# Graph convolution and sparse attention on one core: exponentials at the end of their slots, first-block scores and residual additions one slot later, more values on ScalarE in the last pair

## The chip, the core and the metric

The kernel runs on one core of a Trainium2 chip. A core has TensorE (PE) for matrix products and transposes, VectorE (DVE), ScalarE (ACT), GpSimd (POOL) and SyncE (SP), each with its own queue of instructions, and DMA engines that all queues share. The metric is the device time of one launch in microseconds (us), the median of several runs.

## The reference

`x` has 8 batches of 2048 nodes with 256 features; `adj` is a 2048 by 2048 adjacency matrix, sparse, with its densest rows and columns at the front. Layer 0 is a graph convolution with two linear layers and batch norms, layer 1 an attention with 4 heads that looks only at neighbours. Each is added to its input and layer-normalised. The change touches layer 1 and the end of layer 0 (the second batch norm, the addition and the layer norm), all of which the attention part of the kernel does.

```python
def _L1_gnn_ref(h, W, adj):
    qkv = h @ W
    qkv = qkv.reshape(Bn, Nn, 3, H, HEAD_DIM).transpose(2, 0, 3, 1, 4)
    q, k, v = (qkv[0], qkv[1], qkv[2])
    mask = jnp.where(adj == 0, -jnp.inf, 0.0)
    scores = jnp.einsum('bhid,bhjd->bhij', q, k) / np.sqrt(HEAD_DIM) + mask
    attn = jax.nn.softmax(scores, axis=-1)
    out = jnp.einsum('bhij,bhjd->bhid', attn, v)
    return out.transpose(0, 2, 1, 3).reshape(Bn, Nn, OUT_DIM)
# --- layer 0 ---
x = _layernorm(x + _L0_gnn_ref(x, adj, ...), axis=-1)
# --- layer 1 ---
x = _layernorm(x + _L1_gnn_ref(x, L1_gnn_W, adj), axis=-1)
```

## The kernel before

Everything is in 32-bit floats. The first part of the program builds lists of neighbours and computes layer 0 up to its second batch norm; its result lies in DRAM as `y_d`. The rest is the function `attention`, which this document is about.

**Two kinds of work.** The batches are taken in four pairs. For each pair a *projection* makes queries, keys and values; and a *gather loop* over 132 tiles does the sparse attention of the blocks of 128 query rows 1 to 15. Block 0, whose rows have the most neighbours, is done densely inside the projection. The projection of pair 0 runs alone first. Then the gather loop of pair p runs together with the projection of pair p+1, and the last pair's gather loop runs alone. That makes 528 tiles in all.

**The gather loop.** One turn of the loop is called a slot; slot n issues, in this order: `score(n+4)`, `weigh_values(n+3)`, `add_up(n)`, `gather(n+10)`, then what the projection has for this slot, then what is due later (`finish_block`, `out_stats`, `out_root`, `out_shift`, `emit`).
- `gather` has POOL start an indirect DMA that brings 128 rows of keys and values of both batches into `kg` (10 buffers), and for a tile of left-over edges a second one that brings queries (`qg`). The first tile of a block also loads its queries on SP (`qb`).
- `score` has DVE multiply queries and keys (L1100) and sum per head (L1102), and ACT take the exponential (L1107) into `pw`; for tiles of left-over edges DVE makes a one-hot matrix `oh` (L1110).
- `weigh_values` multiplies the values by the exponentials: on DVE as one instruction (L1126), or, where n % 5 is in `ON_ACT`, that is 1 or 3, on ACT as eight (L1121).
- `add_up` has PE add the weighted values to the block's sums in PSUM (L1140).
- `finish` has DVE divide by the sums (L992 to L996) and POOL add the input (L1002); the layer norm of the result follows.

**The projection.** It works by units of 512 rows of one batch, eight to a pair. Unit k starts at slot s = 14 k (9 k for pair 0, which runs alone), and `at` puts each of its functions into a slot. `bn` (ACT, L853) applies layer 0's batch norm at s. `norm` at s+1 and s+2 transposes half of y on PE into a PSUM tile `pm` (L863), and DVE adds x (L867) and takes statistics (L809, L811). `root`, `shift` and `apply` (POOL, DVE, ACT) do the layer norm, `turn` (PE L889, ACT L894) transposes the result. Then, for each of four tiles of 128 rows, starting at u = s+9 plus 0, 3, 7 or 10: `keys_values` at u (PE L911, ACT L925 and L926), `queries` at u+1 (PE L911, ACT L930), `turn_keys` at u+2 (PE L935, ACT L939), `scores0` of block 0 at u+3 (PE L948, two `pm` tiles), `mask0_scores` at u+4 (DVE L957, ACT L962) and `weigh` at u+6 (PE L970). `store` (SP L979, L983) writes keys, values and queries to DRAM at the last u+3; the next pair's first gather needs them.

**What sets the order.** The order of each queue is the order in which the program text issues its instructions: nothing is rearranged, and the projection's functions stand in their slot in the order in which `at` was called (an earlier unit's first). Each queue runs by itself and waits by semaphores for what an instruction reads, and for the buffer that it writes to be free. The buffers that matter here: `pm`, three PSUM tiles shared by all of the projection's PE work; `pw` and `wv`, five each; `s`, three; `kt` and `p0`, two.

Of the kernel before, what the change touches and what calls it, by code (L numbers as in the profile page):

```python
# [8 lines left out]
F32 = mybir.dt.float32  # L9
# [3 lines left out]
AF = mybir.ActivationFunctionType  # L13
# [4 lines left out]
NHEADS = 4  # L18
# [19 lines left out]
def tile_gcn_then_masked_attention(  # L38
# [15 lines left out]
    nc = tc.nc  # L54
    ENG = mybir.EngineType
    PSUM = bass.MemoryType.PSUM
    P = 128
    B, N, D = x.shape
# [9 lines left out]
    TPC = CH // P  # L68
# [372 lines left out]
    with tc.tile_pool(name="l0", bufs=1, side="right", reuse_waits="tile") as lp, tc.tile_pool(  # L441
# [126 lines left out]
        for n in range(len(tiles)):  # L568
            t, r, col, e = tiles[n]
# [262 lines left out]
    def attention():  # L832

        with ExitStack() as st:
# [4 lines left out]
            ps_m = enter(tc.tile_pool(name="ps_m", bufs=3, space=PSUM, reuse_waits="tile"))  # L839
            enter(tc.manual_schedule(engines=ALL4))  # L840

            x1, yt, x1t, ln, lo, kvr, qr, kt, q0, s0, p0, po0 = ({} for _ in range(12))

            def load(b, c):
                yt[b, c] = ip.tile([P, NO, CH], F32, name="yt")
# [9 lines left out]
                        bias=sh2[:, o : o + 1], scale=sc2[:, o : o + 1],  # L855
                    )

            def norm(b, c, half):
                pm = ps_m.tile([P, IT, D], F32, name="pm")
                for i in range(IT):  # L860
                    r0 = (IT * half + i) * P
                    for o in range(NO):
                        nc.tensor.transpose(  # L863
                            pm[:, i, o * P : (o + 1) * P], yt[b, c][:, o, r0 : r0 + P], ident
                        )
                t = x1[b, c][:, IT * half : IT * (half + 1)]
                nc.vector.tensor_add(t, pm, t)  # L867
                if not half:
                    ln[b, c] = LayerNorm(ip, x1[b, c])
                ln[b, c].stats(range(IT * half, IT * (half + 1)))  # L870
# [152 lines left out]
            def projection(p, step):  # L1023

                slots = {}

                def at(s, f, *args):
                    slots.setdefault(s, []).append((f, args))

                units = [(b, c) for b in range(p * G2, (p + 1) * G2) for c in range(NCH)]  # L1030
                for k, (b, c) in enumerate(units):
                    s = k * step
                    at(max(0, s - step), load, b, c)
                    at(s, bn, b, c)
                    at(s + 1, norm, b, c, 0)
                    at(s + 2, norm, b, c, 1)
                    at(s + 3, root, b, c)
                    at(s + 4, shift, b, c)
                    at(s + 5, apply, b, c, 0)
                    at(s + 6, apply, b, c, 1)  # L1040
                    at(s + 7, turn, b, c, 0)
                    at(s + 8, turn, b, c, 1)
                    if not c:
                        at(s + 9, first_queries, b)
                    for i in range(TPC):
                        u = s + 9 + (step * i) // TPC
                        at(u, keys_values, b, c, i)
                        at(u + 1, queries, b, c, i)
                        at(u + 2, turn_keys, b, c, i)
                        at(u + 3, scores0, b, c, i)  # L1050
                        at(u + 4, mask0_scores, b, c, i)
                        at(u + 6, weigh, b, c, i)
                    at(u + 3, store, b, c)
                    if c == NCH - 1:
                        at(u + 7, lambda b=b: finish(b, 1, 0, po0.pop(b)[:, None]))
                        at(u + 9, out_stats, b, 1, 0)
                return slots

            slots = projection(0, 9)
# [6 lines left out]
            NG = len(tiles)  # L1066
            LEAD = 10
            AHEAD = 4
            ON_ACT = (1, 3)
            kg, qg, qb, oh, pw, wv, po = ({} for _ in range(7))  # L1070

            def load_q(p, t):
                qb[p, t] = ep.tile([P, G2, D], F32, name="qb", bufs=3)
# [21 lines left out]
            def score(n):  # L1095
                p, g = divmod(n, NG)
                t, r, col, e = tiles[g]
                q = qb[p, t] if e < 0 else qg.pop(n)
                pr = ep.tile([P, G2, D], F32, name="pr")
                nc.vector.tensor_mul(pr, q, kg[n][:, :, :D])  # L1100
                s = ep.tile([P, G2, NHEADS], F32, name="s", bufs=3)
                nc.vector.tensor_reduce(  # L1102
                    s.rearrange("p b h -> p (b h)"),
                    pr.rearrange("p b (h e) -> p (b h) e", e=HD), AX.X, ALU.add,
                )
                pw[n] = ep.tile([P, G2, NHEADS], F32, name="pw", bufs=5)
                nc.scalar.activation(pw[n], s, AF.Exp, bias=padb[:, col : col + 1])  # L1107
                if e >= 0:
                    oh[n] = ep.tile([P, P], F32, name="oh", bufs=4)
                    nc.vector.tensor_scalar(  # L1110
                        oh[n], iota_q1, qi1[:, e : e + 1], None, op0=ALU.is_equal
                    )

            def weigh_values(n):
                wv[n] = ep.tile([P, G2, NHEADS * VW], F32, name="wv", bufs=5)
                k, w = kg.pop(n), pw.pop(n)
                if n % 5 in ON_ACT:
                    for b in range(G2):
                        for h in range(NHEADS):
                            hs = slice(h * VW, (h + 1) * VW)  # L1120
                            nc.scalar.activation(  # L1121
                                wv[n][:, b, hs], k[:, b, D:][:, hs], AF.Copy,
                                scale=w[:, b, h : h + 1],
                            )
                    return
                nc.vector.tensor_mul(  # L1126
                    wv[n].rearrange("p b (h e) -> p b h e", e=VW),
                    k[:, :, D:].rearrange("p b (h e) -> p b h e", e=VW),
                    w[:, :, :, None].to_broadcast([P, G2, NHEADS, VW]),
                )  # L1130
# [22 lines left out]
            def at(n, f, *args):  # L1153
                later.setdefault(n, []).append((f, args))
# [3 lines left out]
                gather(n)  # L1158
            for n in range(AHEAD):
                score(n)  # L1160
                if n:
                    weigh_values(n - 1)
            for n in range(NALL_G):
# [12 lines left out]
                    f(*args)  # L1176
                for f, args in later.pop(n, ()):
                    f(*args)
                if r == ELL[t] + CAP[t] - 1:
                    at(n + 1, finish_block, p, t)  # L1180
                    at(n + 3, out_stats, p * G2, G2, t)
                    if t % TPC == TPC - 1:
                        for b in range(p * G2, (p + 1) * G2):
                            u = n + 4 + 2 * (b % G2)
                            at(u, out_root, b, t // TPC)
                            at(u + 1, out_shift, b, t // TPC)
                            for half in range(2):
                                at(u + 2 + half, emit, b, t // TPC, half)
# [19 lines left out]
    class Layer1Input:  # L1208
# [37 lines left out]
        def turn_y(self, b, c, half, pm):  # L1246
            y = self.yt[b, c]
            for i in range(IT):
                r0 = (IT * half + i) * P
                for o in range(NO):  # L1250
                    nc.tensor.transpose(
                        pm[:, i, o * P : (o + 1) * P], y[:, o, r0 : r0 + P], ident
                    )
# [310 lines left out]
```

## Time and profile before

| what | value |
|---|---|
| median of 3 runs (lowest to highest) | 2800.45 us (2800.2 to 2802.91) |
| the profiled execution's own time | 2723.71 us |
| its span | 2721.9 us |
| busy PE, DVE, ACT, POOL over the span | 84%, 70%, 45%, 52% |
| granted TensorE clock, mean | 0.921 |
| L1100 and L1102, DVE, a tile | 0.70 and 0.69 us |
| L1126, weighting on DVE, a tile | 0.73 us |
| L1121, weighting on ACT, one of eight | 0.34 us |
| L1107, exponential on ACT | 0.30 us |
| first gather, last gather | 1303.0 us, 2689.9 us |

The page and the views of one trace are read so: busy times are sums over an engine's instructions, and instructions of one engine may overlap slightly at their ends, so that eight L1121 take about 2.0 us from the first start to the last end. A wait is the idle time just before an instruction, with the instruction that ended it. All times count from the start of the span of this one execution, which was shorter than the runs without a profile.

### The profile page before, as it was taken

The page shows a single profiled execution, that of the slowest core. Times are in us where ns is not written, and L with a number is a line of the kernel's source. Part 1 is how long each engine was busy: PE and PEld are TensorE (multiplying, and loading weights), DVE is VectorE, ACT ScalarE, POOL GpSimd, SP SyncE. Part 2 cuts the span into 40 slices and gives each one's busy share as a digit, 9 for nine tenths or more (in the row PEclk, how much of TensorE's full clock was granted, in tenths as well). Part 3 has the DMA queues.
Part 4 walks back from the last instruction along what each step waited for, and adds up shares of the span by engine and source line. Part 5 has one row for each costly group of instructions (what it writes and reads, how often), then busy time and mean ns, then how long its engine had stood idle before and what let it go on. Part 6 is the DMA issues. An engine that isn't in the chain of part 4 may idle for free.

```text
span 2721.9 us, 29515 instructions
## 1 busy us (share of the span) xinstructions
PE 2295.2 (84%) x8636; PEld 1364.2 (50%) x8636; DVE 1914.8 (70%) x3801; ACT 1227.6 (45%) x3664; POOL 1418.5 (52%) x1481
## 2 busy tenths in 40 slices
PE   6998989889998999799688887888887988966675
PEld 2444444344443444466466665656665666644443
DVE  7966343345439666432688889788798888889997
ACT  6210111011101555355466755766765666755554
POOL 3225435344312577200656657656567566677775
PEclk7999989899989999899798998999998999988777
DMA  9867556467633673332977879878888878889985
GB/s 363 289 253 296 214 199 243 163 223 250 224 110 131 263 263 138 135 117 86 334 267 276 308 269 336 315 252 301 310 304 294 315 261 305 289 281 335 320 310 181
DMA packets 235723, 689.02 MB, mean 253 GB/s; under 512 B 25632, under 2 KB 91680, under 8 KB 213024
## 3 DMA queue, kind: packets, MB, share of 16 engines
q0 software_dynamic: 109248, 442.68, 46.2%
q1 hardware_dynamic: 124000, 227.58, 23.0%
q10 hardware_dynamic: 2304, 16.78, 1.5%
q8 instruction: 71, 1.16, 0.2%
q14 instruction: 100, 0.82, 0.1%
HBM read 556.67 MB, written 130.29 MB: 252 GB/s over the span
## 4 chain that ended last, share of the span: by engine, by line
PE 49%; DVE 24%; ACT 12%; issue 7%; DMA 4%; POOL 3%; SPq 1%; ACTq 0%; POOLq 0%; DVEq 0%
PE pa L588 15%; PE pm L911 7%; PE pa L679 7%; DVE pr L1100 6%; PE ph L469 5%; ACT wv L1121 5%; PE pa L426 4%; DVE s L1102 4%; DVE wv L1126 4%; PE po L1140 3%; ACT x L825 2%; PE pm L948 2%; DVE ln_st L809 1%; PE pm L863 1%; DVE x L867 1%
## 5 line engine op out<-in xcount | busy, mean ns | idle before, releaser
L1084 POOL DMA_INDIRECT kg<-kv_d,idx x528 | 566.9, 1074 | 172.1 <-issue 91.1
L1140 PE MATMUL po<-wv,ident 128*128 128x260 f32 x1472 | 449.2, 433 | 100.6 <-ACT wv L1121 66.1
L588 PE MATMUL pa<-e,wt 128*128 128x512 f32 x928 | 437.6, 620 | 11.3 <-DVE e L327 10.7
L1121 ACT ACTIVATE wv<-kg,pw 128x65 f32<-128x65 f32 x1688 | 425.1, 337 | 0.1
L911 PE MATMUL pm<-wq,x1t 128*128 128x512 f32 (+1 forms) x1024 | 406.2, 521 | 10.4 <-DVE p L957 8.5
L1140 PEld LDWEIGHTS po<-wv,ident 128*128 128x128 f32 x1472 | 291.8, 213 | 209.7 <-ACT wv L1121 106.8
L1102 DVE TENSOR_REDUCE s<-pr 128x8 f32<-128x512 f32 x528 | 362.1, 686 | 18.3
L1107 ACT ACTIVATE pw<-s,padb 128x8 f32<-128x8 f32 x528 | 157.7, 299 | 392.3 <-DVE s L1102 391.6
L588 PEld LDWEIGHTS pa<-e,wt 128*128 128x128 f32 x928 | 180.9, 200 | 225.6 <-issue 206.6
L1126 DVE TENSOR_TENSOR wv<-kg,pw 128x520 f32<-128x520 f32 x317 | 229.9, 725 | 53.8 <-ACT pw L1107 53.0
L1100 DVE TENSOR_TENSOR pr<-qb,kg 128x512 f32<-128x512 f32 x368 | 257.8, 701 | 7.0 <-DMA kg<-kv_d,idx 6.8
L911 PEld LDWEIGHTS pm<-wq,x1t 128*128 128x128 f32 x1024 | 190.5, 198 | 117.4 <-issue 68.3
L1002 POOL TENSOR_TENSOR x<-z,x 128x256 f32<-128x256 f32 x128 | 111.6, 890 | 241.6 <-DVE z L996 241.3
L1140 PE MATMUL po<-wv,oh 128*128 128x260 f32 x640 | 200.6, 440 | 37.8 <-ACT wv L1121 24.5
L523 POOL DMA_INDIRECT e<-xs_d,idx x116 | 114.7, 989 | 161.1 <-PE pa L588 122.1
L1090 POOL DMA_INDIRECT qg<-q_d,idxq x160 | 164.3, 1027 | 48.8 <-issue 46.9
L1140 PEld LDWEIGHTS po<-wv,oh 128*128 128x128 f32 x640 | 129.4, 217 | 97.9 <-ACT wv L1121 43.6
L948 PE MATMUL pm<-q,kt 64*128 64x128 f32 x1024 | 95.0, 305 | 80.9 <-ACT kt L939 80.1
L304 POOL DMA_INDIRECT av<-in_adj_dram,fidx x116 | 113.3, 977 | 82.7 <-DVE wgt L298 32.6
L957 DVE SCALAR_TENSOR_TENSOR p<-mask,pm 128x256 f32<-128x256 uint8 x256 | 95.3, 413 | 82.4 <-PE pm L948 82.4
L970 PEld LDWEIGHTS po<-kvr,p 128*128 128x128 f32 x1024 | 131.6, 191 | 24.1 <-issue 15.8
L970 PE MATMUL po<-kvr,p 128*128 128x65 f32 x1024 | 129.4, 269 | 9.2 <-ACT p L962 9.2
(196 smaller groups left out, 3478.3 us busy)
## 6 DMA issues: line engine op xcount, KB each, us to landing
kv_d<-kvr SPq DMA_DIRECT2D x32, 1032.0 KB, 8.0
e<-h_d SPq DMA_DIRECT2D x28, 1024.0 KB, 8.1
e<-in_adj_dram SPq DMA_DIRECT2D x16, 1024.0 KB, 19.6
xt<-in_x_dram SPq DMA_DIRECT2D x16, 1024.0 KB, 7.6
xs_d<-xt ACTq DMA_DIRECT2D x16, 1024.0 KB, 7.7
y_d<-y SPq DMA_DIRECT2D x32, 512.0 KB, 2.7
yt<-y_d SPq DMA_DIRECT2D x32, 512.0 KB, 9.1
x<-in_x_dram SPq DMA_DIRECT2D x32, 512.0 KB, 12.9
```

Of the source, the lines that this page charges most:

```text
L588: nc.tensor.matmul(pa[:, c, :], w, xg[n].t[:, c * CH : (c + 1) * CH], start=(r == 0), stop=(r == ELL[t] + CAP[t] - 1),)
L679: nc.tensor.matmul(py, w[:, f, :], t[:, f, :], start=(f == 0), stop=(f == 1))
L911: nc.tensor.matmul(pm, x1t[b, c][:, d, i * P : (i + 1) * P], rhs(d), start=(d == 0), stop=(d == ND - 1),)
L970: nc.tensor.matmul(po0[b][:, h, :], p[:, h % 2, h // 2, :], heads(kvr[b, c][:, i, D:])[:, h, :], start=(j == 0 and h == 0), stop=(j == NT ...
L1084: nc.gpsimd.indirect_dma_start(out=kg[n].rearrange("p b e -> p (b e)"), out_offset=None, in_=kv_d[p][:], in_offset=bass.IndirectOffsetOnAx ...
L1090: nc.gpsimd.indirect_dma_start(out=qg[n].rearrange("p b e -> p (b e)"), out_offset=None, in_=q_d[p][:], in_offset=bass.IndirectOffsetOnAxi ...
L1100: nc.vector.tensor_mul(pr, q, kg[n][:, :, :D])
L1102: nc.vector.tensor_reduce(s.rearrange("p b h -> p (b h)"), pr.rearrange("p b (h e) -> p (b h) e", e=HD), AX.X, ALU.add,)
L1107: nc.scalar.activation(pw[n], s, AF.Exp, bias=padb[:, col : col + 1])
L1121: nc.scalar.activation(wv[n][:, b, hs], k[:, b, D:][:, hs], AF.Copy, scale=w[:, b, h : h + 1],)
L1126: nc.vector.tensor_mul(wv[n].rearrange("p b (h e) -> p b h e", e=VW), k[:, :, D:].rearrange("p b (h e) -> p b h e", e=VW), w[:, :, :, None ...
L1140: nc.tensor.matmul(po[p, t][:, b, : NHEADS * VW], lhs, w[:, b, :], start=(r == 0), stop=(r == ELL[t] + CAP[t] - 1),)
```

## The change

Four things are altered, all in `attention`.

1. `norm` is split. `turn_y` (the transposes) keeps its slots s+1 and s+2; the addition and its statistics come one slot after it, at s+2 and s+3, and everything of the unit that follows, from `root` to the stores and the end of block 0, one slot later than before. A transposed half is kept in `ys` until then.
2. `scores0`, `mask0_scores` and `weigh` come at u+4, u+5 and u+7, so the scores follow two slots after the keys are turned, not one.
3. The exponential is taken out of `score` into `exps`, which is issued at the end of the slot, after the weighting of the tile before, the gather and the projection's and later work.
4. For the last pair (n at least 396) `weigh_values` uses `LAST_ON_ACT`: ACT weighs where n % 5 is 0, 2 or 4, DVE where it is 1 or 3.

```diff
@@ -839,7 +839,7 @@
             ps_m = enter(tc.tile_pool(name="ps_m", bufs=3, space=PSUM, reuse_waits="tile"))
             enter(tc.manual_schedule(engines=ALL4))
 
-            x1, yt, x1t, ln, lo, kvr, qr, kt, q0, s0, p0, po0 = ({} for _ in range(12))
+            x1, yt, x1t, ln, lo, kvr, qr, kt, q0, s0, p0, po0, ys = ({} for _ in range(13))
 
             def load(b, c):
                 yt[b, c] = ip.tile([P, NO, CH], F32, name="yt")
@@ -855,16 +855,18 @@
                         bias=sh2[:, o : o + 1], scale=sc2[:, o : o + 1],
                     )
 
-            def norm(b, c, half):
-                pm = ps_m.tile([P, IT, D], F32, name="pm")
+            def turn_y(b, c, half):
+                pm = ys[b, c, half] = ps_m.tile([P, IT, D], F32, name="pm")
                 for i in range(IT):
                     r0 = (IT * half + i) * P
                     for o in range(NO):
                         nc.tensor.transpose(
                             pm[:, i, o * P : (o + 1) * P], yt[b, c][:, o, r0 : r0 + P], ident
                         )
+
+            def norm(b, c, half):
                 t = x1[b, c][:, IT * half : IT * (half + 1)]
-                nc.vector.tensor_add(t, pm, t)
+                nc.vector.tensor_add(t, ys.pop((b, c, half)), t)
                 if not half:
                     ln[b, c] = LayerNorm(ip, x1[b, c])
                 ln[b, c].stats(range(IT * half, IT * (half + 1)))
@@ -1032,28 +1034,29 @@
                     s = k * step
                     at(max(0, s - step), load, b, c)
                     at(s, bn, b, c)
-                    at(s + 1, norm, b, c, 0)
-                    at(s + 2, norm, b, c, 1)
-                    at(s + 3, root, b, c)
-                    at(s + 4, shift, b, c)
-                    at(s + 5, apply, b, c, 0)
-                    at(s + 6, apply, b, c, 1)
-                    at(s + 7, turn, b, c, 0)
-                    at(s + 8, turn, b, c, 1)
+                    for half in range(2):
+                        at(s + 1 + half, turn_y, b, c, half)
+                        at(s + 2 + half, norm, b, c, half)
+                    at(s + 4, root, b, c)
+                    at(s + 5, shift, b, c)
+                    at(s + 6, apply, b, c, 0)
+                    at(s + 7, apply, b, c, 1)
+                    at(s + 8, turn, b, c, 0)
+                    at(s + 9, turn, b, c, 1)
                     if not c:
-                        at(s + 9, first_queries, b)
+                        at(s + 10, first_queries, b)
                     for i in range(TPC):
-                        u = s + 9 + (step * i) // TPC
+                        u = s + 10 + (step * i) // TPC
                         at(u, keys_values, b, c, i)
                         at(u + 1, queries, b, c, i)
                         at(u + 2, turn_keys, b, c, i)
-                        at(u + 3, scores0, b, c, i)
-                        at(u + 4, mask0_scores, b, c, i)
-                        at(u + 6, weigh, b, c, i)
+                        at(u + 4, scores0, b, c, i)
+                        at(u + 5, mask0_scores, b, c, i)
+                        at(u + 7, weigh, b, c, i)
                     at(u + 3, store, b, c)
                     if c == NCH - 1:
-                        at(u + 7, lambda b=b: finish(b, 1, 0, po0.pop(b)[:, None]))
-                        at(u + 9, out_stats, b, 1, 0)
+                        at(u + 8, lambda b=b: finish(b, 1, 0, po0.pop(b)[:, None]))
+                        at(u + 10, out_stats, b, 1, 0)
                 return slots
 
             slots = projection(0, 9)
@@ -1066,8 +1069,8 @@
             NG = len(tiles)
             LEAD = 10
             AHEAD = 4
-            ON_ACT = (1, 3)
-            kg, qg, qb, oh, pw, wv, po = ({} for _ in range(7))
+            ON_ACT, LAST_ON_ACT = (1, 3), (0, 2, 4)
+            kg, qg, qb, oh, sc, pw, wv, po = ({} for _ in range(8))
 
             def load_q(p, t):
                 qb[p, t] = ep.tile([P, G2, D], F32, name="qb", bufs=3)
@@ -1103,18 +1106,22 @@
                     s.rearrange("p b h -> p (b h)"),
                     pr.rearrange("p b (h e) -> p (b h) e", e=HD), AX.X, ALU.add,
                 )
-                pw[n] = ep.tile([P, G2, NHEADS], F32, name="pw", bufs=5)
-                nc.scalar.activation(pw[n], s, AF.Exp, bias=padb[:, col : col + 1])
+                sc[n] = s
                 if e >= 0:
                     oh[n] = ep.tile([P, P], F32, name="oh", bufs=4)
                     nc.vector.tensor_scalar(
                         oh[n], iota_q1, qi1[:, e : e + 1], None, op0=ALU.is_equal
                     )
 
+            def exps(n):
+                col = tiles[n % NG][2]
+                pw[n] = ep.tile([P, G2, NHEADS], F32, name="pw", bufs=5)
+                nc.scalar.activation(pw[n], sc.pop(n), AF.Exp, bias=padb[:, col : col + 1])
+
             def weigh_values(n):
                 wv[n] = ep.tile([P, G2, NHEADS * VW], F32, name="wv", bufs=5)
                 k, w = kg.pop(n), pw.pop(n)
-                if n % 5 in ON_ACT:
+                if n % 5 in (LAST_ON_ACT if n >= (NP - 1) * NG else ON_ACT):
                     for b in range(G2):
                         for h in range(NHEADS):
                             hs = slice(h * VW, (h + 1) * VW)
@@ -1158,6 +1165,7 @@
                 gather(n)
             for n in range(AHEAD):
                 score(n)
+                exps(n)
                 if n:
                     weigh_values(n - 1)
             for n in range(NALL_G):
@@ -1176,6 +1184,8 @@
                     f(*args)
                 for f, args in later.pop(n, ()):
                     f(*args)
+                if n + AHEAD < NALL_G:
+                    exps(n + AHEAD)
                 if r == ELL[t] + CAP[t] - 1:
                     at(n + 1, finish_block, p, t)
                     at(n + 3, out_stats, p * G2, G2, t)
```

## The prediction

> **What bounds the kernel now.** I read the page first for shares and slices, then the busy times by stage (one row per stretch of the span), then the waits of each engine in the stages that the change touches, then single episodes in the timeline. Attention starts near 1110 us. By the first gather (1303.0 us) the projection of pair 0 is done; three pairs are then gathered while the next pair is projected (1303 to 2396), and the last pair is gathered alone (2396 to 2709).
>
> ```profile
> core 0: us, PE busy (x) PEld busy (x) DVE busy (x) ACT busy (x) POOL busy (x), PEclk, DMA share, GB/s
> 1110.00:1303.00 193.00, 171.19 (x981) 116.43 (x979) 59.96 (x175) 96.64 (x226) 14.43 (x54) 0.96 0.36 124
> ...
> 1303.00:2396.00 1093.00, 903.42 (x4456) 657.27 (x4458) 927.34 (x1931) 702.14 (x2394) 695.42 (x793) 0.93 0.84 296
> 2396.00:2709.00 313.00, 208.98 (x588) 127.87 (x586) 285.73 (x542) 160.97 (x620) 231.60 (x229) 0.79 0.84 294
> ```
>
> Columns: length, then busy us of PE, PE's weight loads, DVE, ACT, POOL, then TensorE's clock, DMA share, GB/s. In the first stretch PE is the bound (171 of 193 us). In the three shared pairs DVE (927 of 1093, 85%) and PE (903, 83%) are close to each other and neither is full: about 166 us of DVE time is waiting. In the last pair DVE is the bound (286 of 313, 91%). DVE's waits, in the shared pairs:
>
> ```profile
> engine line waited for: us in total, times, longest us
> DVE x L867 <- PE pm L863: 61.2, 42, 3.5
> DVE wv L1126 <- ACT pw L1107: 52.7, 45, 4.7
> DVE lo_nm L819 <- POOL lo_rs L140: 7.2, 7, 2.0
> DVE pr L1100 <- DMA kg<-kv_d,idx: 6.3, 1, 6.3
> ```
>
> Two waits hold 114 of those 166 us: the residual addition waiting for its transposes, and the weighting of values waiting for its exponentials. PE and ACT, in the same stretch:
>
> ```profile
> PE pm L948 <- ACT kt L939: 79.6, 52, 4.5
> PE pm L863 <- DVE p L957: 37.7, 21, 2.9
> ...
> ACT pw L1107 <- DVE s L1102: 246.0, 125, 11.3
> ACT kvr L925 <- PE pm L911: 95.9, 53, 4.8
> ```
>
> ACT stands 246 us at an exponential, first in its slot, while DVE still forms the sum; PE stands 80 us at first-block scores whose keys ACT copies one slot earlier. One episode shows how they lock:
>
> ```profile
> 1482.49 0.74 DVE L957 SCALAR_TENSOR_TENSOR p<-mask,pm 128x256 f32<-128x256 uint8 x2
> ...
> 1482.96 0.66 PE L863 MATMUL pm<-ident,yt 128*128 128x128 f32 x4 [0.85 <-DVE p L957]
> ...
> 1483.65 0.69 DVE L867 TENSOR_TENSOR x<-pm,x 128x512 f32<-128x512 f32 x1 [0.42 <-PE pm L863]
> ```
>
> PE can't transpose until DVE's masking frees a `pm` buffer, and DVE's next instruction waits for exactly that transpose.
>
> **What the Trainium skill says.** "PSUM — Partial Sum Buffer", section "Engine vs sequencer instructions": the queues of ScalarE, VectorE and GpSimd are strictly first in, first out. The episode agrees: behind L867 all of DVE stood still. So the place of an instruction in its queue is a cost by itself, and that is what most of this change alters. "Perfetto Trace Analysis", section "Optimizing Scalar/DVE Operations": with DVE saturated, moving work to ScalarE may make sense. The last pair's row (DVE 91%, ACT 51%) is that case. No other page is needed.
>
> **The change, part by part.** The profiled execution took 2723.71 us (span 2721.9); the runs' median is 2800.45, 77 us more, which the profile doesn't explain. I carry the change in us over to the median.
>
> (a) Residual addition a slot later (`turn_y` at s+1, `norm` at s+2, and all that follows a slot later). The transposes are now a whole slot ahead of their reader. A slot lasts 1093/396 = 2.76 us; transposes of a half took 0.66 us after at most one masking. So the 61.2 us wait should nearly go; I keep 5. But `pm` has three buffers, and one is now held across a slot boundary. Following the new order through a unit of 14 slots, a new same-slot wait appears: two score buffers and the second transposed half fill all three, so `keys_values` of the third tile can start only after DVE's second addition of that slot. Queued behind it on PE are the next slot's value sums, whose slack is three slots; on ACT the copies of keys and values. That leads to (c).
>
> (b) First-block scores two slots after their keys. PE's 79.6 us at L948 should almost vanish. PE isn't the fuller engine, and DVE loses only 4.2 us to PE at the masking now, so I book nothing. What replaces it late is the same-slot buffer wait (masking, then the next `pm`), which exists before too (37.7 and 8.5 us of PE).
>
> (c) Exponentials at the end of the slot. No instruction is added. ACT gets to the slot's values and copies without the 246 us stand; but each exponential now sits behind that slot's copies from PE. DVE's L1126 of the next slot needs it 1.37 us (product and sum, starts 0.7 apart) after that slot begins. Worst chain, from (a): addition ends, PE 1.98, ACT copies 0.72, exponential 0.30, hand-overs 0.1 = 3.1 us, against DVE's statistics, product and sum, 2.2 us: 0.9 us late. Behind a masking with a query product: 1.03 + 0.37 + 0.30 + 0.1 = 1.8 against 1.37: 0.4 late. Behind masking with keys turned and `turn`: 0.6 late. A key-value product whose slot is PE's fullest (sums, weighting, scores and product, 4.5 us at the page's durations) comes 1.3 late; two others 0.3. Sum per unit 0.9 + 2x0.4 + 0.6 + 1.3 + 2x0.3 = 4.2 us, and only the 60% of tiles that DVE weighs feel it: 2.5 us, x24 units = 60 us against 52.7 now: +7. Ends: 10 us (ACT's head start hides all: -43) and 120 us (+67, twice my lateness).
>
> (d) The stores of keys, values and queries, the block-0 finish and its statistics move a slot too. On SP the store goes from s+22 to s+23; loads of the next unit keep their slots and come first in the first stretch. At a pair's end the first gather needs the last store, and POOL already stands there: 5.9, 3.5 and 6.9 us before the three later pairs, followed before the last pair by DVE 5.06 us behind POOL's addition (L1002). A slot later costs POOL up to 2.8 us more; the gather is six slots ahead of its score, 16 us, less 6.3 landing, less the stand: little is left. I take +2 each, +6 (0 to +10).
>
> (e) Last pair: positions 0, 2, 4 of five instead of 1, 3. Of tiles 396 to 527, 79 go to ACT instead of 53: 26 fewer L1126 on DVE, which cost 0.61 us start to start (0.72 in the row): -16 to -19. ACT takes 26 x 1.92 to 2.02 = 50 to 53 more, from 161 to 213 of some 300: hidden, two neighbouring ones take 4.4 of two slots' 4.7. What is late next is POOL: 231.6 busy, plus 42 of pauses between gathers that nothing ends and 12 of 0.3 us ones, is 286 of 313; the rest, 23, is waiting for DVE's quotients. So POOL gives way by at most 27, and DMA is 84 to 91% busy there. I take -12 (-19 to -3). The final chain stays: the last tile moves to ACT (2.0 for 0.7) but no longer waits for its neighbour's.
>
> (f) First stretch: PE's work is unchanged and it is the bound; 0 (-4 to +5).
>
> (g) Pass-through. With 61 us of stalls gone DVE would be 88% busy, PE 86%, DMA 88%, so other waits will lengthen. I return 15 of (a)'s 56.
>
> Sum: (a) -56+15, (c) +7, (d) +6, (e) -12, (f) 0 = -40 us; I allow (b) and ACT's head start -6, so -46: 2678 for the profiled execution, 2754 for the median.
>
> **Rivals.** R1, the exponentials eat the gain: (c) reaches its bad end of 120 us and (a) is only balanced: -56+15+67+6-12 = +20 at worst, middle of the way about -9: 2791. For it: the new order puts 4 key-value and 4 query copies per unit ahead of an exponential; PE is 83% busy, so seldom early. Against: ACT now starts a slot's work about 1.4 us earlier.
>
> R2, slower: a closed loop DVE masking or addition, PE product, ACT copy, exponential, DVE weighting, one turn per slot. Place: the seven late slots per unit; with 60% on DVE that is 7 x 0.6 x 24 = 101 weightings. It decides once these wait (52.7 + 46 + 7)/101, about 1.0 us each, on average; my list gives 0.6. At 1.5 us: 152 - 60 = +92, so -46+92 = +46: 2846. For it: only three `pm` buffers, one now held longer. Against: the lateness isn't carried over, as PE has 9.6 us of work in the 11 us between two such locks.
>
> R3, only the last pair fails to gain, because POOL's gathers bind it: -34: 2766. It lies inside the forecast's range.
>
> That the change doesn't do what it says is excluded: the instruction order of the changed program shows each of the moves, and ScalarE loads one table in both.
>
> **How the numbers follow.** Forecast (with R3) 0.62; R1 0.16; R2 0.22. A measurement of this kernel tells about 0.2% from no change, 5.6 us. The forecast's cases all lie beyond that on the fast side; R1 splits 0.09 faster, 0.06 same, 0.01 slower. So faster 0.71, same 0.06, slower 0.23. The forecast's own range, from the ends of (a) to (f), is 2720 to 2785; with R1 and the near part of R2, leaving out about 0.15 above and 0.04 below, 2717 to 2816.
>
> **What would show it.** Right: L867 waiting for L863 under 10 us; PE at L948 waiting for keys under 20; ACT's wait for the sum well under 246; the stretch of shared pairs 1050 to 1065 us with DVE about 88% busy; the last pair about 300 with L1126 there at some 58 and POOL's waits for quotients under 23. Wrong: L1126 waiting for exponentials above 115 us (R1) or 155 (R2), PE waiting for the second addition at L911, or the last pair as long as before. A stand at the pairs' ends that grows by more than 10 us in all would break (d).

## The result, and the profile after

The changed kernel takes 2805.88 us (median of 20 runs, 2794.02 to 2814.62), the kernel before 2800.99 us in the same series (20 runs, 2795.55 to 2811.58): a ratio of 1.0014, 95% interval 1.0002 to 1.0026. Five microseconds were lost where 46 were forecast as a gain.

The kernel before takes about 2724 us in some series of runs and 2786 to 2802 us in others; its profile, on which the prediction rests, is of the first kind, the profile after (span 2802.3 us) of the second, and the 77 us that the prediction left unexplained are most likely this difference. So ratios below always stand between runs of one series, and times of the two profiles are not subtracted from each other.

The busy times by stage of the changed kernel, with the columns of the prediction's first fence:

```profile
0.00:1304.00 1304.00, 1184.11 (x3594) 578.81 (x3594) 699.68 (x1324) 359.96 (x642) 494.56 (x460) 0.95 0.57 209
1304.00:2480.00 1176.00, 944.37 (x4435) 682.92 (x4436) 922.38 (x1920) 715.17 (x2384) 690.57 (x791) 0.90 0.80 275
2480.00:2803.00 323.00, 205.29 (x608) 126.39 (x608) 275.73 (x533) 224.31 (x847) 233.82 (x232) 0.81 0.84 291
```

The first stretch is as long as before: the first gather starts at 1303.9 us, before at 1303.0. In the last pair 227 more instructions run on ACT than before (847 for 620, in a window 10 us longer); 208 of them are the new share of ACT, eight for each of 26 tiles. The shared pairs are the trouble: DVE does 922 us of work in 1176, 78%, where the prediction wanted 88% of 1050 to 1065. The waits of DVE in that stretch:

```profile
DVE wv L1133 <- ACT pw L1119: 180.1, 97, 10.3
DVE wv L1133 <- issue: 13.0, 8, 4.4
...
DVE lo_nm L819 <- POOL lo_rs L140: 5.2, 7, 1.4
```

The residual addition (now L869) no longer appears: that wait is gone, as meant. But the weighting (L1133, before L1126) waits 180 us for exponentials, 97 times and up to 10.3 us; in the profile before it was 52.7 us, at most 4.7. Ten of the 97, the eight longest among them, contain a stand of ACT whose releaser the trace doesn't know (last section). These ten hold 58 of the 180 us; the longest of the others is 4.2 us. ACT and PE in the same stretch:

```profile
ACT kvr L927 <- PE pm L913: 207.3, 71, 10.1
ACT p L964 <- DVE p L959: 82.5, 57, 2.6
ACT pw L1119 <- DVE s L1105: 56.5, 36, 10.8
```

```profile
PE pm L913 <- DVE x L869: 36.2, 16, 4.3
...
PE pm L891 <- DVE p L959: 34.0, 20, 2.8
```

ACT's 246 us at the exponential fell to 57. In exchange ACT now stands 207 us at the copies of keys and values, waiting for PE's products (before 96), and 82.5 us at the exponentials of block 0, waiting for DVE's masks (before 18); the moved exponential is queued behind both. One episode in the timeline of the changed kernel shows it (start, length, instruction; in brackets the idle time before it):

```profile
1503.58 1.98 PE L913 MATMUL pm<-wq,x1t 128*128 128x512 f32 x4
1504.06 0.69 DVE L1105 TENSOR_REDUCE s<-pr 128x8 f32<-128x512 f32 x1
...
1505.60 0.37 ACT L927 COPY kvr<-pm 128x256 f32<-128x256 f32 x1 [5.40 <-PE pm L913]
...
1506.13 0.31 ACT L1119 ACTIVATE pw<-s,padb 128x8 f32<-128x8 f32 x1
...
1506.48 2.03 ACT L1128 ACTIVATE wv<-kg,pw 128x65 f32<-128x65 f32 x8
...
1508.41 0.61 ACT L964 ACTIVATE p<-p 128x512 f32<-128x512 f32 x1
1508.93 0.36 ACT L932 ACTIVATE qr<-pm 128x256 f32<-128x256 f32 x1
...
1509.20 0.28 ACT L1119 ACTIVATE pw<-s,padb 128x8 f32<-128x8 f32 x1
...
1509.51 0.70 DVE L1133 TENSOR_TENSOR wv<-kg,pw 128x520 f32<-128x520 f32 x1 [1.75 <-ACT pw L1119]
```

The sum for the last exponential is ready at 1504.75. Its exponential starts at 1509.20, 4.45 us later: ACT first stands for PE's product, then does the copies, the exponential of the tile before, that tile's eight values (2.03 us), the block-0 exponentials (one instruction) and a copy of queries. DVE has meanwhile done the next product and sum, and stands for 1.75 us. In the old place the exponential would have been queued ahead of the eight values, the block-0 exponential and the copy of queries, which belong to its slot, but still behind the copies of keys and values of the slot before.

### The profile page after: what moved, and what is told of

It is laid out like the page before. It is cut to its first block, busy times and chain, and to the rows that moved or that the text cites. A ratio compares the mean times of both kernels' runs of the same rounds, so it can differ in the third digit from the quotient of the medians.

```text
span 2802.3 us, 29764 instructions
## 1 busy us (share of the span) xinstructions
PE 2333.8 (83%) x8636; PEld 1388.1 (50%) x8636; DVE 1897.8 (68%) x3775; ACT 1299.4 (46%) x3872; POOL 1419.0 (51%) x1481
## 4 chain that ended last, share of the span: by engine, by line
PE 53%; DVE 18%; ACT 11%; issue 8%; DMA 4%; POOL 4%; another core or an unknown queue 2%; SPq 1%; ACTq 0%; POOLq 0%; DVEq 0%
PE pa L588 14%; PE pm L913 10%; PE pa L679 6%; PE po L1147 6%; PE ph L469 5%; ACT wv L1128 4%; PE pa L426 4%; DVE pr L1103 4%; DVE wv L1133 3%; DVE s L1105 2%; PE po L972 2%; ACT x L825 2%; POOL kg L1087 2%; PE pm L950 1%
## 5 line engine op out<-in xcount | busy, mean ns | idle before, releaser
L1147 PE MATMUL po<-wv,ident 128*128 128x260 f32 x1472 | 455.8, 437 | 98.7 <-DVE wv L1133 49.4
L1128 ACT ACTIVATE wv<-kg,pw 128x65 f32<-128x65 f32 x1896 | 480.6, 336 | 20.2 <-remote 7.2
L913 PE MATMUL pm<-wq,x1t 128*128 128x512 f32 (+1 forms) x1024 | 415.0, 532 | 66.4 <-DVE x L869 36.2
L1147 PEld LDWEIGHTS po<-wv,ident 128*128 128x128 f32 x1472 | 301.1, 216 | 227.5 <-issue 64.1
L1133 DVE TENSOR_TENSOR wv<-kg,pw 128x520 f32<-128x520 f32 x291 | 212.4, 730 | 225.8 <-ACT pw L1119 186.9
L1147 PE MATMUL po<-wv,oh 128*128 128x260 f32 x640 | 209.7, 455 | 36.1 <-DVE wv L1133 26.4
L927 ACT COPY kvr<-pm 128x256 f32<-128x256 f32 x128 | 47.5, 371 | 268.6 <-PE pm L913 248.3
```

Of the source, the lines that this page charges most:

```text
L913: nc.tensor.matmul(pm, x1t[b, c][:, d, i * P : (i + 1) * P], rhs(d), start=(d == 0), stop=(d == ND - 1),)
L1128: nc.scalar.activation(wv[n][:, b, hs], k[:, b, D:][:, hs], AF.Copy, scale=w[:, b, h : h + 1],)
L1133: nc.vector.tensor_mul(wv[n].rearrange("p b (h e) -> p b h e", e=VW), k[:, :, D:].rearrange("p b (h e) -> p b h e", e=VW), w[:, :, :, None ...
L1147: nc.tensor.matmul(po[p, t][:, b, : NHEADS * VW], lhs, w[:, b, :], start=(r == 0), stop=(r == ELL[t] + CAP[t] - 1),)
```

## The experiments

All ratios are against the kernel before, run in the same series. There are five series; the kernel before took 2723.47, 2785.78, 2723.99, 2802.38 and 2802.23 us in them.

**First series: the change taken apart.** The kernel before again, unaltered, as a base for the waits in this series:

> The kernel before, unaltered, for another profile of it. Its shown profile (2723.71 us) lies 72 us under the fastest of its 20 runs (2795.55), while the changed kernel's profile (2804.0) lies among its own. Theory A (the shown execution is typical in kind, only quick): a new profile near 2800 has the same waits, each a little larger: residual addition for its transposes about 61 us in the shared pairs, weighting for exponentials 53 to 70. Theory B (the stall was not there in the usual execution): the residual addition waits under 30 us, and the extra 77 us stand in other waits, most likely weighting for exponentials above 100.

2723.23 us, the same as its neighbours (2723.47); in its trace the addition waits 64.6 us for its transposes, the weighting 50.1 us for exponentials. Then the last pair's new share alone:

```diff
-            ON_ACT = (1, 3)
+            ON_ACT, LAST_ON_ACT = (1, 3), (0, 2, 4)
...
-                if n % 5 in ON_ACT:
+                if n % 5 in (LAST_ON_ACT if n >= (NP - 1) * NG else ON_ACT):
```

> Only the last pair's positions 0, 2, 4 on ScalarE. Both theories: 5 to 15 us faster than before (ratio 0.995 to 0.998), the last pair's stretch shorter by that. Rival (POOL binds the last pair): under 3 us, with POOL's waits for DVE's quotients shrinking and DVE's waits for gathers appearing.

2714.67 us, ratio 0.9967 [0.9954, 0.998]: 9 us gained. Then the exponentials at the end of their slots alone, on the kernel before:

```diff
-                pw[n] = ep.tile([P, G2, NHEADS], F32, name="pw", bufs=5)
-                nc.scalar.activation(pw[n], s, AF.Exp, bias=padb[:, col : col + 1])
+                sc[n] = s
...
+            def exps(n):
+                col = tiles[n % NG][2]
+                pw[n] = ep.tile([P, G2, NHEADS], F32, name="pw", bufs=5)
+                nc.scalar.activation(pw[n], sc.pop(n), AF.Exp, bias=padb[:, col : col + 1])
...
                 for f, args in later.pop(n, ()):
                     f(*args)
+                if n + AHEAD < NALL_G:
+                    exps(n + AHEAD)
```

> Only the exponentials moved to the end of their slots. Theory A (they sit behind the same slot's copies from PE and eat what the other parts gain): 30 to 80 us slower (ratio 1.01 to 1.03), weighting waiting for exponentials above 150 us in the shared pairs. Theory B (the other parts gain nothing, the exponentials cost little): within 15 us of before.

2738.09 us, ratio 1.0053 [1.0032, 1.0073]. Its DVE waits, 1303 to 2360 us:

```profile
DVE wv L1130 <- ACT pw L1116: 118.1, 80, 5.4
DVE x L867 <- PE pm L863: 11.2, 26, 0.8
```

and two of its ACT waits:

```profile
ACT p L962 <- DVE p L957: 155.4, 69, 6.4
ACT pw L1116 <- DVE s L1102: 95.2, 69, 11.4
```

So the move by itself does two things: the wait for exponentials more than doubles (50 to 118 us), and the residual addition's wait nearly goes (65 to 11 us), without that addition having been moved. The two nearly cancel: 68 us more, 53 less, and 15 us of time. Why the addition's wait goes isn't shown; DVE itself may come to it later, held up at weightings before it. ACT's stand at the exponential fell as well (from 246 us in the profile before to 95 here), but ACT gained little by it: it now stands 155 us (18 in the profile before) at the exponentials of block 0, for DVE's masks, with the moved exponential queued behind them. Last, the slots alone (residual addition and scores later, exponentials in their old place, old share in the last pair): the change without the edits of the two diffs above.

> Only the residual additions and the first-block scores one slot later, exponentials in their old place, old positions in the last pair. Theory A: 25 to 60 us faster (ratio 0.978 to 0.991), residual addition waiting under 10 us. Theory B: within 10 us of before, since what the addition waited for is then waited for elsewhere.

2642.62 us, ratio 0.9699 [0.9677, 0.9721]: 81 us gained, twice what the prediction gave to these steps. DVE's waits in this kernel:

```profile
DVE wv L1129 <- ACT pw L1110: 33.3, 41, 2.6
...
DVE x L869 <- PE pm L863: 5.3, 5, 1.5
```

Both waits are low. The parts in this series multiply to 0.9699 x 0.9967 x 1.0053 = 0.9718, not 1.0014. Either they don't add up, or the series of the whole differs in more than the time of the kernel before; the next series go after that.

**Second series: where in the slot the exponential costs.** The whole change once more:

> The changed kernel, unaltered, on the experiments' chip if the kernel before takes about 2723 us there as in the last runs. Parts alone gave -81 (slots), +15 (exponentials), -9 (last pair). Theory C (the parts add up, and the result's chip was different): about 2650 us, ratio 0.973. Theory D (the exponentials cost far more once additions and scores are a slot later, because then the same-slot copies from PE are late): 2715 to 2735, ratio about 1.00, weighting waiting for exponentials above 150 us in the shared pairs against 33 with the slots alone.

2797.62 us, ratio 1.0037 [1.002, 1.0053]. The whole change with the exponential back in `score`, and nothing else altered:

> The changed kernel with the exponentials back in score: slots and last pair together. Both theories: the sum of the parts, -81 - 9 = -90, ratio 0.967, about 2633 us. If the last pair's gain is used up by an earlier arrival there: 0.970.

2689.97 us, ratio 0.9653 [0.9628, 0.9678]: in one series, 108 us less than the whole change. DVE's wait for exponentials from 1304 to 2360 us is 43.9 us (42 times, at most 3.2) in this kernel and 150.9 (81 times, at most 10.3) in the whole change: 107 us more, about the whole of the loss. Between the two places, the exponential right after the weighting of the tile before, ahead of the sums and of the projection's copies:

```diff
                 if n + AHEAD - 1 < NALL_G:
                     weigh_values(n + AHEAD - 1)
+                if n + AHEAD < NALL_G:
+                    exps(n + AHEAD)
                 add_up(n)
...
-                if n + AHEAD < NALL_G:
-                    exps(n + AHEAD)
```

> The changed kernel with the exponential directly after weigh_values, ahead of the projection's work, not at the end. Theory D (the copies from PE ahead of it are the cost): like e5 within 15 us, ratio 0.966 to 0.972, weighting waiting for exponentials under 60 us. Rival (the eight value instructions ahead of it are the cost): stays near e4, 0.99 to 1.00.

2732.72 us, ratio 0.9806 [0.978, 0.9833]; the wait is 99.8 us (58 times, at most 7.3). That is neither of the two outcomes expected but between them: behind the eight values alone the exponential costs 43 us, behind the rest of the slot's work on ACT another 65. Then the residual addition a slot later with the scores of block 0 at their old distance, so the slots' gain can be divided. Against the kernel with slots alone:

```diff
-                        at(u + 4, scores0, b, c, i)
-                        at(u + 5, mask0_scores, b, c, i)
-                        at(u + 7, weigh, b, c, i)
+                        at(u + 3, scores0, b, c, i)
+                        at(u + 4, mask0_scores, b, c, i)
+                        at(u + 6, weigh, b, c, i)
...
-                        at(u + 8, lambda b=b: finish(b, 1, 0, po0.pop(b)[:, None]))
-                        at(u + 10, out_stats, b, 1, 0)
+                        at(u + 7, lambda b=b: finish(b, 1, 0, po0.pop(b)[:, None]))
+                        at(u + 9, out_stats, b, 1, 0)
```

> Slots alone, but first-block scores at u+3 as before: only the residual additions and all that follows a slot later. If the forecast's step (b) is right that the scores bring nothing: as the slots alone, 0.970. If the later scores bring a part, because PE then runs ahead of ACT: 0.980 to 0.990, PE at the scores waiting for keys about 60 to 80 us.

2724.4 us, ratio 0.9766 [0.9742, 0.979]: 61 us of the gain belong to the addition. Here PE still waits 44.9 us for keys at L950, and DVE 69.8 us for exponentials.

**Third series: the deadline moved too.** If the cost is that the exponential misses the weighting of the next slot, the weighting a slot later must remove it, with the exponential still last. On the whole change:

```diff
-                if n:
-                    weigh_values(n - 1)
+                if n > 1:
+                    weigh_values(n - 2)
...
-                if n + AHEAD - 1 < NALL_G:
-                    weigh_values(n + AHEAD - 1)
+                if n + AHEAD - 2 < NALL_G:
+                    weigh_values(n + AHEAD - 2)
```

> The changed kernel with the exponentials still at the end of their slots, but the weighting of values one slot later, so that an exponential has a whole slot more before DVE needs it. Theory D (the deadline is the cost: the exponential comes late for the next slot's weighting): most of what the move costs comes back, ratio 0.965 to 0.98, weighting waiting for exponentials under 60 us in the shared pairs. Rival (ACT is simply delayed by standing for PE's copies, and the values it weighs itself are late for PE): stays at 0.995 to 1.005.

2634.95 us, ratio 0.9669 [0.9654, 0.9684]. DVE's wait, 1304 to 2360 us:

```profile
DVE wv L1133 <- ACT pw L1119: 32.6, 42, 2.0
```

The exponentials alone again, in this series:

> The exponentials alone once more. On the chip of the first runs (before 2723 us) they cost 0.53%; on top of the other two parts they cost 4.0% on a chip where before takes 2786. If the other chip is the reason: ratio 1.03 to 1.05 where before takes about 2786 to 2800. If the other parts are the reason (interaction): 1.003 to 1.010 again.

2738.58 us, ratio 1.0062 [1.0048, 1.0075], with the same waits as the first time (114.0 us at the weighting, 11.0 at the addition). And the scores of block 0 a slot later alone, on the kernel before:

```diff
-                        at(u + 3, scores0, b, c, i)
-                        at(u + 4, mask0_scores, b, c, i)
-                        at(u + 6, weigh, b, c, i)
+                        at(u + 4, scores0, b, c, i)
+                        at(u + 5, mask0_scores, b, c, i)
+                        at(u + 7, weigh, b, c, i)
...
-                        at(u + 7, lambda b=b: finish(b, 1, 0, po0.pop(b)[:, None]))
-                        at(u + 9, out_stats, b, 1, 0)
+                        at(u + 8, lambda b=b: finish(b, 1, 0, po0.pop(b)[:, None]))
+                        at(u + 10, out_stats, b, 1, 0)
```

> First-block scores at u+4, masking at u+5, weighting at u+7 with everything else as before. If the later scores bring a gain of their own (as the addition alone, 0.977, against both, 0.970, hints): 0.985 to 0.995, PE at the scores waiting for keys under 20 us. If they help only together with the later addition: within 0.3% of before.

2756.34 us, ratio 1.0116 [1.0101, 1.0132]: slower by 32 us, although PE's wait for keys is gone; neither expectation allowed for that. DVE's waits:

```profile
DVE x L867 <- PE pm L863: 106.4, 42, 5.7
DVE wv L1126 <- ACT pw L1107: 28.3, 31, 2.6
```

Against the kernel before in this series (next run), the weighting gains 21 us and the addition loses 42: with the scores moved, the transposes that DVE waits for in the same slot come later still. The scores' new slot is worth something only once the addition no longer waits in the slot of its transposes. The kernel before, a third time, closed the series:

> The kernel before, unaltered, for a profile on this chip. If before takes 2780 or more here: the first 1303 us as in the shown profile within 5 us, and the rest spread over the gather loops, with gathers or instruction fetch later than there. If it takes about 2723: the same profile again.

2724.51 us against 2723.99, with 64.7 us at the addition and 49.6 at the weighting.

**Fourth and fifth series: does the loss come with the series or with the parts?** Up to here the exponentials alone had been measured only where the kernel before takes 2724 us, and the whole only where it takes 2786 or more. So whole and parts where it takes 2802 us. Whole, whole without the exponentials' move, and the latter with the weighting a slot later:

> The changed kernel, unaltered, hoped for on a chip where before takes about 2724. Interaction (the exponentials' move takes away the same wait of the residual addition as the slots do, so on top of the slots only its own cost is left): ratio 0.995 to 1.01 there too, 2710 to 2750. The slow chip's doing: the parts add up there, 0.97 to 0.98, 2640 to 2670.

> Slots and last pair, exponentials in score, beside e12 on the same chip. Either way 0.963 to 0.970. The difference to e12 is the price of the exponentials' place on top of the rest: 25 to 40 thousandths under interaction, 5 under the chip's doing.

> As e13, with the weighting a slot later as in e8. If e8's gain was the deadline alone, a later weighting has nothing to give here where the exponentials are early: 0.962 to 0.970, as e13. If a later weighting is good by itself: 0.955 or lower.

2807.82 us, 1.0014 [1.0002, 1.0026]; 2711.62 us, 0.9674 [0.9656, 0.9692]; 2692.32 us, 0.9617 [0.9596, 0.9637]. In one series, then, the exponentials' place costs 96 us on top of slots and last pair. The stage rows of the whole and of the one without the move, over one and the same stretch:

```profile
1304.00:2360.00 1056.00, 842.04 (x3901) 609.69 (x3902) 818.04 (x1705) 630.91 (x2110) 611.63 (x701) 0.89 0.79 274
```

```profile
1304.00:2360.00 1056.00, 885.60 (x4284) 640.26 (x4285) 893.08 (x1866) 675.30 (x2303) 676.39 (x764) 0.92 0.84 298
```

and their waits at the weighting, in the same order:

```profile
DVE wv L1133 <- ACT pw L1119: 152.2, 84, 10.6
```

```profile
DVE wv L1129 <- ACT pw L1110: 69.2, 38, 6.9
```

In equal time the second kernel gets 161 DVE instructions further (1866 for 1705), and DVE's busy share goes from 77% to 85%; the wait at the weighting is 83 us shorter. TensorE's granted clock is also higher, 0.92 for 0.89, and a matmul takes 207 ns (885.60/4284) for 216. Whether the lower clock follows from the stands or adds to them, no run separates. As an estimate from these rows, 9 ns on 4284 matmuls are 39 us of PE's work, so at most that much of the 96 us could be the clock's. The exponentials alone, the whole, and the whole with the later weighting:

> The exponentials alone, beside the whole change (e16) on one chip. If before takes about 2724 here: 1.006 again. If it takes 2786 to 2802: interaction says 1.003 to 1.012, the chip's doing says 1.03 to 1.05.

> The whole change beside e15. If before takes about 2724 here: interaction says 0.99 to 1.01, the chip's doing 0.97 to 0.98. If it takes 2786 to 2802: 1.001 to 1.004 as measured twice.

> The whole change with the weighting a slot later (e8). If before takes 2786 to 2802 here: 0.960 to 0.972 if the deadline is the cost there as well, above 0.985 if the slow chip has another cost. If it takes about 2724: 0.967 again.

2812.89 us, 1.0033 [1.0021, 1.0044]; 2806.71 us, 1.0013 [0.9998, 1.0027]; 2681.28 us, 0.9562 [0.9538, 0.9585]. So where the kernel before takes 2802 us, too, the move alone costs 11 us (0.33%), and 96 on top of the other parts. The parts explain the loss without a difference between the series; whether the whole loses as much where the kernel before takes 2724 us was not run. The last kernel is the best of the study and beats both the kernel before and the changed one by more than 4%. Not all of that is the deadline: with the exponentials in their old place the later weighting still gave 19 us (0.9674 to 0.9617). And once the weighting comes later, the exponentials' new place gains a little instead of costing 96 us: 0.9562 against 0.9617, each against the kernel before in its own series.

## Why the prediction was wrong

The time lies in the range on record, but at the far side of it from the forecast, and the sign is wrong. That it lies inside is luck: two terms were missed by much, in opposite directions. Step by step:

- **(c), the exponentials, is the step that failed.** It was priced at +7 us: 60 us of waiting at the weighting in place of 52.7. In the whole change it waits 180 us in the shared pairs, and taking this one edit back gains 96 us (fourth series) or 108 us (second series). Two things were wrong in its working. The list of late slots counted PE's product and the copy ahead of the exponential, not the eight value activations, which the episode shows at 2.03 us and which stand ahead of it whenever ACT weighs the tile before; the exponential behind these alone costs 43 us. And the bad end was set at twice a mean lateness of 0.6 us, as if every slot began on time. The 97 waits have a mean of 180.1/97 = 1.9 us, or 1.4 without the ten that contain a stand of unknown cause. Alone, the edit cost 11 to 15 us, near the +7; it is in the new order of the slots that the price was wrong.
- **R2's mechanism fits the waits best**, beyond its point of decision of about 1.0 us: DVE's addition and masking release PE (36 us at the key-value product, 34 at the transposes of `turn`), PE's product releases ACT's copy (207 us), the exponential behind that copy releases DVE's weighting (180 us). "The lateness isn't carried over" was the argument against it. Four waits of 3.3 to 4.2 us, none with a stand of unknown cause, are longer than a slot (1176/396 = 2.97 us) and speak against that argument. That the loop closes on itself is read from these waits, not shown; no run broke the loop at PE alone. R2's price for the exponentials, 7 + 92 = 99 us, is close to the 96 and 108 measured. Its 2846 us was too slow because (a) and (b) brought about 40 us more than it assumed.
- **(a) was right in kind and too small.** The addition's wait went from 64.6 to 5.3 us. With (g) handed back and (d) added it was booked at -56+15+6 = -35; alone it gave -61 (second series), with the scores -81 (first). The 15 us of (g), returned for other waits, were not there to return: the weighting's wait fell as well, from 50 to 33 us.
- **(b) was booked at nothing and has two signs.** Alone it costs 32 us; on top of (a) it gains: the ratio goes from 0.9766 with the addition alone to 0.9653 with scores and last pair, and the last pair was worth 0.33% in the first series, so about 0.8%, some 22 us. The prediction treated parts of one loop as terms of a sum.
- **(a) and (c) take away the same wait.** With the exponentials' move alone, 53 of the addition's 65 us are already gone. Once the slots have taken them, only the move's price is left. That is the larger part of why two edits of -81 and +15 us (first series) end at no gain. The rest is that the price itself grows: the weighting's wait rises by 68 us with the move alone (first series) and by 107 on top of the slots (second).
- **(d) cost nothing that shows**: the stands before the first gather of the three later pairs were 5.9, 3.5 and 6.9 us before, 5.8, 5.2 and 5.9 with the slots alone; +6 was booked.
- **(e) was right**: -12 booked, -9 measured alone, within -19 to -3. (Its sum for POOL leaves 27 of the 313 us, not the 23 that it names as the rest; nothing hangs on it.) **(f) was right**: the first stretch did not change.
- Of the signs that were named, those for the slots came true (L867's wait under 10 us, PE's wait at first-block scores under 20, ACT's wait for the sum well under 246); that for the shared pairs, 1050 to 1065 us at 88% of DVE, did not. Two that were to show it wrong came as well: the weighting's wait above 155 us, and PE waiting for the addition at the key-value product (36.2 us).

The Trainium skill's rule that the prediction cited, strict order in the queues of ScalarE and VectorE ("PSUM — Partial Sum Buffer", section "Engine vs sequencer instructions"), agrees with the 4.45 us of the episode. It was applied to what stands behind the moved instruction, and too little to what then stands ahead of it.

## What to carry to other kernels

Moving an instruction to the end of its slot removes the stand before it, and gives it the lateness of everything that is now ahead of it in the queue; in this kernel it paid only once its reader's deadline moved by a slot too (1.0013 to 0.9562 in one series). Edits that remove the same wait don't add up, and edits in one loop of engines can change sign with each other: run each alone and the whole without each, in one series. When a sum of parts is wanted, ask of each part which wait it ends, and which other part has already ended that one.

## What the runs showed of the hardware

The kernel with the later weighting took 2634.95 us in the third series and 2681.28 in the fifth, and the difference lies after 1304 us: up to there PE is busy for 1188.72 and 1188.60 us. Whether the chip makes it isn't known: the second and the third series bear the same chip number on record, while the kernel before takes 2785.78 and 2723.99 us in them. In the series of the result, the second, the fourth and the fifth, ACT stands for PE's results with a releaser that the trace doesn't know ("remote"), in the kernel with the exponentials alone from 1304 to 2360 us:

```profile
ACT x1t L894 <- remote: 30.0, 6, 6.3
ACT kvr L925 <- remote: 22.6, 3, 8.8
```

In no trace of the first and third series, nor in the profile before, does ACT have one such wait; in those of the other series there are 8 to 17 of them, 31 to 70 us in all, and none before 1304 us. In the changed kernel eleven of them last over 2 us, and during ten of these the DMA engines are busy for 0.99 or more of the time, where the mean of the shared pairs is 0.80. Stretches as full occur without such waits as well (45 of 125 stretches of 8 us in the profile before, 1310 to 2310 us), so this is a lead and not a cause. The longest wait of DVE in the changed kernel is one of them handed on (its timeline):

```profile
2313.28 0.69 DVE L1105 TENSOR_REDUCE s<-pr 128x8 f32<-128x512 f32 x1
...
2315.72 1.16 PE L903 MATMUL pm<-x1t,wq 128*128 128x128 f32 x8
...
2320.78 0.38 ACT L908 ACTIVATE q<-pm 128x256 f32<-128x256 f32 x1 [5.69 <-remote]
...
2321.22 3.63 PE L913 MATMUL pm<-wq,x1t 128*128 128x512 f32 x4 [4.34 <-ACT q L908]
...
2324.89 0.37 ACT L927 COPY kvr<-pm 128x256 f32<-128x256 f32 x1 [3.72 <-PE pm L913]
...
2325.42 0.31 ACT L1119 ACTIVATE pw<-s,padb 128x8 f32<-128x8 f32 x1
...
2325.77 0.70 DVE L1133 TENSOR_TENSOR wv<-kg,pw 128x520 f32<-128x520 f32 x1 [10.29 <-ACT pw L1119]
```

The queries' product ends at 2316.88 by the trace, and its copy starts at 2320.78. The next product takes 3.63 us, where it took 1.98 in the episode above: TensorE's granted clock is 0.57 from 2321 to 2325 us and was 1.00 from 1503 to 1506, and 1.98/0.57 = 3.5, so the clock accounts for nearly all of that. The exponential, whose sum was ready at 2313.97, shares in both. The late copy isn't settled; the clock is 1.00 from 2316 to 2321 us. In the Trainium skill, "Perfetto Trace Analysis", section "Tensor Engine Instruction (MATMUL, LD_WEIGHTS)", says that the end of a matmul in the profile is computed and not observed, so the product may really have run longer, or its result may have come late; no run here tells which. The kernel before was not profiled in a series with these waits, nor the whole change run in one without.
